# Sixteen-head attention: the row sums from weights whose two key tiles GpSimd has added, and three pieces of work moved in the order

## The chip, the cores and the metric

The kernel runs on one NeuronCore of a Trainium2 chip. A core has TensorE (PE, matrix products into the accumulators, PSUM), VectorE (DVE), ScalarE (ACT), GpSimd (POOL) and SyncE (SP, which here only issues DMAs). Each takes its own list of instructions in order and waits on semaphores for the others. The metric is the device time of one execution in microseconds (us).

## The reference

A decoder of four blocks, each of self-attention, cross-attention and a feed-forward part, on x of 8 batch rows x 256 positions x 256 features. After every part comes `x = layernorm(x + part(x))`. The change touches the self-attention of the first three blocks, parts 0, 3 and 6 of the twelve. All have 16 heads of 16 features:

```python
q, k, v = x @ Wq + bq, x @ Wk + bk, x @ Wv + bv       # split into 16 heads of 16
scores  = q @ k.T * 0.25                              # part 3 adds slope[h] * (j - i), part 6 masks j > i
out     = softmax(scores) @ v                         # per head
x       = layernorm(x + out @ Wo + bo)
```

Part 0 has biases, part 3 (ALiBi) biases and the distance term, part 6 (causal) the mask and no biases. The other nine parts are not touched.

## The kernel before

`attention16` (line 341 on) computes the three parts. A **block** is one batch row b and one half c of the heads (8 heads on 128 partitions, a head in each 16-wide strip), 16 blocks in all, in the order (b, 0), (b, 1). Two blocks of the same b are called a period below.

A block takes four **steps**, units `(e, u)` of `UNITS`. `step(i, s)` puts onto TensorE, alternately, the scores of one unit of the *next* block (tile `s`, queries on the partitions) and the scores of one unit of *this* block turned round (tile `t`, keys on the partitions). The scores `s` serve only to find each query's largest score: VectorE takes the maximum (`dve.tensor_reduce` into `nm`). The turned scores `t` already have that maximum subtracted, through an extra row of the queries (`qm`), so ScalarE takes their exponential straight into `eT` (line 460). An `eT` tile holds, for two heads, two key tiles of 128 keys by 256 queries. In part 6 VectorE first adds the mask and GpSimd clears the half above the diagonal of `eT` (line 466). `s` and `t` are two-bank PSUM tiles of one tag with two buffers, so a step's tiles reuse those of the step before.

`attend(i, e, whats)` multiplies `eT` by the values (`what` 0, `vp`) and by a matrix of ones (`what` 1), the latter giving each query's sum of weights, both into one PSUM tile `av`. For each it runs over k = 0, 1 (the two key tiles) and four heads. Each product of 32-bit data shows as two instructions in the trace, so values are 16 instructions and sums 16. `normalise(i, half)` takes the reciprocal of the sums and multiplies on VectorE, 128 queries at a time, into `aT`.

Around the steps stands work for the neighbours, as filler for TensorE: the projections of the next b (`project_qk` for keys and queries, `proj_tok` for values), the output projection of the last one, the turning of the maxima (`turn_maxima`, `less_max` gives `qm`), the residual (`add_x`; its `xb = x + bo` is GpSimd's), the layer norm (`norm_stats`, with a power on GpSimd, then `norm_scaled`) and the transposition of the new x (`finish`). `leave_qk` brings projected queries or keys out of PSUM, twice each with different strips: on ScalarE in parts 0 and 6, on VectorE in part 3 (`masked`, with `tabs`).

The order on TensorE and VectorE is that of the text: `order_of_text` (line 142) chains every `matmul`, `transpose` and `dve` operation to the one before it on its engine. The lists of ScalarE, GpSimd and SyncE are laid out by the framework's scheduler when the program is built; GpSimd's also holds work of later parts, such as the bias products of part 3 (`bm`, line 816). The loop at lines 526 to 568 is the order around the change; there the functions named above are called between `step(i, 0)` and `step(i, 3)`.

## Time and profile before

| what | value |
|---|---|
| runs | 3790.48, 3794.57, 3794.21 us; median 3794.21 |
| the profiled execution | 3791.73 us, its span 3789.9 us, mean granted TensorE clock 0.978 |
| part 0, 20 to 262 us | busy: TensorE 217.5, VectorE 154.3, ScalarE 99.4, GpSimd 19.7 us |
| part 3, 1040 to 1262 us | TensorE 204.7, VectorE 167.7, ScalarE 70.0, GpSimd 14.1 us |
| part 6, 1770 to 2000 us | TensorE 201.5, VectorE 177.4, ScalarE 80.0, GpSimd 55.9 us |
| products with `vp` and with `ones`, three parts | 1536 instructions each |
| waits of TensorE's scores `s` for the maximum `nm`, 60 to 230 us | 5.5 us in 7 waits |

In the profile's lines a group is given by its line in the kernel, engine, operation, `out<-in` by tile names and shape, then busy time and mean time of one, then the idle time before it and what ended it. Lines 151, 156 and 159 are the helpers through which VectorE's operations and TensorE's products and transpositions go, so there the tile names tell the groups apart. In the timeline a row has its start, its length, the engine (PEld is TensorE's loading of the stationary operand), what it does and, in brackets, the idle time before it and what ended that. The table by stretches gives busy time and number of instructions for PE, PEld, DVE, ACT and POOL, then the granted clock and the share of the DMA engines.

### The profile page before, as it was taken

The page shows a single profiled execution, that of the slowest core. Times are in us where ns is not written, and L with a number is a line of the kernel's source. Part 1 is how long each engine was busy: PE and PEld are TensorE (multiplying, and loading weights), DVE is VectorE, ACT ScalarE, POOL GpSimd, SP SyncE. Part 2 cuts the span into 40 slices and gives each one's busy share as a digit, 9 for nine tenths or more (in the row PEclk, how much of TensorE's full clock was granted, in tenths as well). Part 3 has the DMA queues.
Part 4 walks back from the last instruction along what each step waited for, and adds up shares of the span by engine and source line. Part 5 has one row for each costly group of instructions (what it writes and reads, how often), then busy time and mean ns, then how long its engine had stood idle before and what let it go on. Part 6 is the DMA issues. An engine that isn't in the chain of part 4 may idle for free. (4 is left out here: it accounts for less than half of the span.)

```text
span 3789.9 us, 51235 instructions
## 1 busy us (share of the span) xinstructions
PE 3575.5 (94%) x21130; PEld 2558.6 (68%) x21130; DVE 1730.3 (46%) x3319; ACT 1086.7 (29%) x2615; POOL 853.0 (23%) x900
## 2 busy tenths in 40 slices
PE   7989999999999688999989999999999999999998
PEld 5656555656566465787666766777766777688887
DVE  5753222222478565213874457666664444420003
ACT  3432111111133355322333321343333334321111
POOL 1000000000100366221223320222222333332214
PEclk9998999999999899999999999999999999999999
DMA  7000000001000010342005000100010000035542
GB/s 274 2 15 6 17 17 17 17 17 38 1 1 2 12 56 1 131 164 93 2 2 92 1 23 1 31 1 1 1 31 12 12 11 2 12 131 185 187 164 73
DMA packets 65481, 175.70 MB, mean 46 GB/s; under 512 B 8064, under 2 KB 39552, under 8 KB 52896
## 3 DMA queue, kind: packets, MB, share of 16 engines
q0 software_dynamic: 17280, 98.38, 7.3%
q1 hardware_dynamic: 47968, 74.05, 6.7%
q8 instruction: 166, 2.72, 0.3%
q14 instruction: 67, 0.55, 0.0%
HBM read 139.12 MB, written 33.29 MB: 45 GB/s over the span
## 5 line engine op out<-in xcount | busy, mean ns | idle before, releaser
L151 DVE TENSOR_REDUCE nm<-s 128x4 f32<-128x1024 f32 (+2 forms) x448 | 455.6, 1030 | 154.5 <-PE s L649 66.5
L597 POOL TENSOR_TENSOR ex<-ex,urc 128x1024 f32<-128x1024 f32 x192 | 363.4, 1893 | 717.0 <-DVE urc L151 626.8
L588 ACT ACTIVATE ex<-s,nm 128x256 f32<-128x256 f32 (+1 forms) x704 | 337.8, 494 | 345.7 <-DVE nm L151 327.1
L460 ACT ACTIVATE eT<-t 128x1024 f32<-128x1024 f32 (+1 forms) x192 | 182.6, 953 | 360.3 <-PE t L156 360.3
L797 PE MATMUL pu<-xT_l,w2a 128*128 128x512 f32 x512 | 244.2, 599 | 0.0
L797 PE MATMUL pg<-xT_l,w2a 128*128 128x512 f32 x512 | 242.0, 594 | 1.1 <-ACT sg L922 1.1
L923 DVE TENSOR_TENSOR h<-pu,sg 128x512 f32<-128x512 f32 x128 | 88.6, 692 | 336.6 <-PE pu L797 336.6
L156 PE MATMUL s<-qk,qk 32*128 32x256 f32 (+1 forms) x1536 | 217.2, 400 | 23.7 <-DVE nm L151 17.9
L922 ACT ACTIVATE sg<-pg 128x512 f32<-128x512 f32 x128 | 76.4, 597 | 565.2 <-PE pg L797 565.2
L782 PE MATMUL py<-w2b,h 128*128 128x256 f32 x1024 | 226.2, 379 | 0.0
L159 PE MATMUL etr<-ident,ex 128*128 128x128 f32 x1568 | 215.0, 279 | 10.5 <-issue 7.1
L782 PEld LDWEIGHTS py<-w2b,h 128*128 128x128 f32 x1024 | 194.6, 190 | 40.1 <-issue 15.3
L159 PEld LDWEIGHTS etr<-ident,ex 128*128 128x128 f32 x1568 | 173.4, 142 | 69.8 <-issue 59.4
L156 PE MATMUL t<-qm,qk 32*128 32x256 f32 (+1 forms) x1536 | 204.6, 387 | 10.9 <-DVE nm L151 9.9
L649 PE MATMUL s<-kg,qg 64*128 64x256 f32 x1280 | 192.5, 403 | 3.3 <-DVE eT L151 2.9
L675 PE MATMUL av<-eT,vg 128*64 128x256 f32 x1280 | 189.3, 395 | 4.3 <-DVE eT L151 2.8
L156 PEld LDWEIGHTS s<-qk,qk 32*128 32x128 f32 x1536 | 125.7, 190 | 93.7 <-issue 48.9
L789 DVE SCALAR_TENSOR_TENSOR x<-py,g,x 128x256 f32<-128x256 f32 x256 | 110.2, 478 | 166.1 <-PE py L782 165.9
L797 PEld LDWEIGHTS pu<-xT_l,w2a 128*128 128x128 f32 x512 | 98.1, 192 | 122.1 <-issue 122.1
L797 PEld LDWEIGHTS pg<-xT_l,w2a 128*128 128x128 f32 x512 | 97.0, 191 | 108.0 <-issue 105.0
L1501 PE MATMUL ph<-xgT,w11a 128*128 128x256 f32 x736 | 162.8, 379 | 0.5 <-DVE xgT L1530 0.5
L1508 PE MATMUL py<-w11b,h 128*128 128x256 f32 x736 | 162.6, 379 | 0.0
(339 smaller groups left out, 6227.5 us busy)
## 6 DMA issues: line engine op xcount, KB each, us to landing
slots<-zero SPq DMA_DIRECT2D x16, 1024.0 KB, 16.7
given<-yo SPq DMA_DIRECT2D x23, 256.0 KB, 3.0
w2a<-in_L_ffn_Wg SPq DMA_DIRECT2D x8, 512.0 KB, 4.0
w2a<-in_L_ffn_Wu SPq DMA_DIRECT2D x8, 512.0 KB, 4.8
w2b<-in_L_ffn_Wd SPq DMA_DIRECT2D x8, 512.0 KB, 3.9
lines<-w9r SPq DMA_DIRECT2D x1, 4096.0 KB, 44.4
bias<-lines SPq DMA_DIRECT2D x4, 768.0 KB, 7.5
x<-in_x SPq DMA_DIRECT2D x8, 256.0 KB, 5.5
```

The lines of the kernel that those rows point to most:

```text
L151: return lambda *args, **kw: in_order(getattr(nc.vector, op)(*args, **kw))
L156: in_order(nc.tensor.matmul(*args, **kw))
L159: in_order(nc.tensor.transpose(*args))
L460: nc.scalar.activation(eT[:, :, :n], tt[:, :, :n], AF.Exp)
L588: nc.scalar.activation(ex[:, g, :], flat[:, g, :], AF.Exp, bias=nm[:, g:g + 1], accum_out=sums[:, g:g + 1])
L597: nc.gpsimd.tensor_tensor(ex, ex, rc[:, :nseg].unsqueeze(2).to_broadcast([P, nseg, 1024 // nseg]), ALU.mult)
L649: nc.tensor.matmul(st[:, i, q * S:(q + 1) * S], qg[r:r + d, c, q * P:(q + 1) * P], kg[r:r + d, c, :], start=True, stop=True)
L675: nc.tensor.matmul(av[64 * i:64 * i + d, c * S:(c + 1) * S], vg[:, k, (2 * c + i) * d:(2 * c + i + 1) * d], eT[:, (2 * i + k) * S:(2 * i + ...
L782: nc.tensor.matmul(py[:, q * D:(q + 1) * D], h[:, f, i * P:(i + 1) * P], w2[:, f, :], start=(f == 0), stop=(f == nf - 1))
L797: nc.tensor.matmul(ph, w1[:, c, f * P:(f + 1) * P], xT[p][:, c, :], start=(c == 0), stop=(c == 1))
L1501: nc.tensor.matmul(ph[:, i * S:(i + 1) * S], w1[:, c, f * P:(f + 1) * P], srcs[c], start=(c == 0), stop=(c == 1))
L1508: nc.tensor.matmul(py[:, q * D:(q + 1) * D], h[:, f, q * P:(q + 1) * P], w2[:, f, :], start=(f == 0), stop=(f == NF - 1))
```

## The change

In parts 0 and 3, after each exponential, GpSimd adds the two key tiles of `eT` into a new tile `eS` (four buffers). The sums then need one pass over `eS` in place of two over `eT`. Part 6 keeps its sums over both tiles. In all three parts the order changes:

- the sums of the second strip (e = 1) of a block are taken in the next block: after its step 1 where that has c = 0, after its step 0 where c = 1; before, they followed at the end of a block with c = 1, and after the next block's step 0 for one with c = 0;
- the queries' projection of the next b is cut in its two column halves, one after step 1 of c = 0 (with the sums), one after step 0 of c = 1; `leave_qk` and `masked` take the halves `cs` that are to leave;
- in c = 0 both halves of `normalise` come between step 1 and step 2; in c = 1 they stay around step 1;
- `norm_stats` moves from the end of c = 0 to after step 0 of c = 1, `norm_scaled` after step 1 there.

```diff
@@ -366,31 +366,37 @@
 
             blocks = [(b, c) for b in range(B) for c in range(2)]
             qk = {}
-            qms, avs, eTs, aTs, ys = {}, {}, {}, {}, {}
-
-            def masked(dst, src, i):
+            qms, avs, eTs, eSs, aTs, ys = {}, {}, {}, {}, {}, {}
+
+            def masked(dst, src, i, cs):
 
                 scale = hc[:, 4 + i % 2:5 + i % 2] if i < 2 else hc[:, i % 2:i % 2 + 1]
+                dst = dst[:, cs[0]:cs[-1] + 1, :]
                 if tabs is not None:
-                    dve.scalar_tensor_tensor(dst, src, scale, tabs[:, i], ALU.mult, ALU.add)
+                    dve.scalar_tensor_tensor(dst, src, scale, tabs[:, i, cs[0]:cs[-1] + 1, :],
+                                             ALU.mult, ALU.add)
                 elif kbias is not None:
-                    for c in range(2):
-                        nc.scalar.activation(dst[:, c, :], src[:, c, :], AF.Identity, scale=scale,
+                    for j, c in enumerate(cs):
+                        nc.scalar.activation(dst[:, j, :], src[:, j, :], AF.Identity, scale=scale,
                                              bias=kbias[:, 2 * i + c:2 * i + c + 1])
                 elif i < 2:
                     nc.scalar.activation(dst, src, AF.Copy, scale=scale)
                 else:
                     nc.scalar.activation(dst, src, AF.Identity, scale=scale, bias=hc[:, i:i + 1])
 
-            def project_qk(b, k):
-                pt = proj_T(wk_ if k else wq, xTb(b), 0, f"p{'qk'[k]}_{li}_{b}")
-                return pt.rearrange("p (c s) -> p c s", c=2)
-
-            def leave_qk(b, k, pt):
+            def project_qk(b, k, cs=(0, 1)):
+                pt = bank("mm", f"p{'qk'[k]}_{li}_{b}_{cs[0]}")
+                for j, c in enumerate(cs):
+                    for i, src in enumerate(xTb(b)):
+                        matmul(pt[:, j * S:(j + 1) * S], (wk_ if k else wq)[:, i, c * P:(c + 1) * P],
+                               src, start=(i == 0), stop=(i == 1))
+                return pt[:, :len(cs) * S].rearrange("p (c s) -> p c s", c=len(cs))
+
+            def leave_qk(b, k, pt, cs=(0, 1)):
                 for i in (2 * k, 2 * k + 1):
-                    tg = wk.tile([P, 2, S], F32, tag=f"qk{i}", name=f"qk{i}_{li}_{b}")
-                    masked(tg, pt, i)
-                    qk[b, i] = tg
+                    if (b, i) not in qk:
+                        qk[b, i] = wk.tile([P, 2, S], F32, tag=f"qk{i}", name=f"qk{i}_{li}_{b}")
+                    masked(qk[b, i], pt, i, cs)
 
             def leave_v(b, pv):
                 vp = vpads[b % 2]
@@ -466,6 +472,11 @@
                             nc.gpsimd.affine_select(out=diag, in_=diag, compare_op=ALU.is_ge,
                                                     fill=0.0, base=0, pattern=[[0, 2], [1, P]],
                                                     channel_multiplier=-1)
+                    else:
+
+                        eS = wk.tile([P, 2, S], F32, tag="eS", name=f"eS_{li}_{b2}_{c2}{e2}{u2}", bufs=4)
+                        nc.gpsimd.tensor_tensor(eS, eT[:, :, 0:S], eT[:, :, S:2 * S], ALU.add)
+                        eSs[i, e2, u2] = eS
                     eTs[i, e2, u2] = eT
 
             def turn_maxima(i):
@@ -490,16 +501,18 @@
                     avs[i] = bank("av", f"av_{li}_{b}_{c}")
                 av, vp = avs[i], vpads[b % 2]
                 for what in whats:
-                    for k in range(2):
+                    for k in range(1 if what == 1 and not causal else 2):
                         for j in range(4):
                             h, r = 8 * c + 2 * j + e, 32 * j
                             q0 = P if causal and k == 1 else 0
                             first = e == 0 and what == 0 and k == 0
+                            if what == 1 and not causal:
+                                src = eSs[i, e, j // 2][:, j % 2, :]
+                            else:
+                                src = eTs[i, e, j // 2][:, j % 2, k * S:k * S + S - q0]
                             matmul(av[r:r + 32, what * S + q0:(what + 1) * S],
-                                   vp[:, k, h, :] if what == 0 else ones[:, e, :],
-                                   eTs[i, e, j // 2][:, j % 2, k * S:k * S + S - q0],
-                                   start=first, stop=e == 1 and what == 1 and k == 1,
-                                   skip_group_check=True)
+                                   vp[:, k, h, :] if what == 0 else ones[:, e, :], src,
+                                   start=first, stop=e == 1 and what == 1, skip_group_check=True)
 
             def normalise(i, half):
 
@@ -526,28 +539,37 @@
                 for i, (b, c) in enumerate(blocks):
                     more = b + 1 < B
                     if c == 0:
-                        step(i, 0, lambda: normalise(i - 1, 0))
-                        normalise(i - 1, 1)
+                        step(i, 0)
                         if more:
                             pk = project_qk(b + 1, 1)
                         step(i, 1)
                         if more:
                             leave_qk(b + 1, 1, pk)
-                            pq = project_qk(b + 1, 0)
+                        if i > 0:
+                            attend(i - 1, 1, (1,))
+                        if more:
+                            pq = project_qk(b + 1, 0, (0,))
+                        for half in range(2):
+                            normalise(i - 1, half)
+                        step(i, 2)
+                        if more:
+                            leave_qk(b + 1, 0, pq, (0,))
                     else:
                         step(i, 0)
                         if b > 0:
+                            ys[b - 1] = norm_stats(b - 1, ys[b - 1], f"l{li}")
+                        attend(i - 1, 1, (1,))
+                        if more:
+                            pq = project_qk(b + 1, 0, (1,))
+                        step(i, 1, lambda: normalise(i - 1, 0))
+                        if b > 0:
                             norm_scaled(ys.pop(b - 1))
-                        attend(i - 1, 1, (1,))
-                        step(i, 1, lambda: normalise(i - 1, 0))
                         normalise(i - 1, 1)
                         if more:
+                            leave_qk(b + 1, 0, pq, (1,))
                             pv = proj_tok(wv, xTb(b + 1), 0, f"pv_{li}_{b + 1}")
-                    step(i, 2)
-                    if more:
-                        if c == 0:
-                            leave_qk(b + 1, 0, pq)
-                        else:
+                        step(i, 2)
+                        if more:
                             leave_v(b + 1, pv)
                     attend(i, 0, (0, 1))
                     step(i, 3)
@@ -560,12 +582,11 @@
                         tr = turn_maxima(i + 1)
                         less_max(i + 1, 0, tr)
                     if b > 0 and c == 0:
-                        y = add_x(wk, b - 1, po, bo, f"{li}_{b - 1}")
+                        ys[b - 1] = add_x(wk, b - 1, po, bo, f"{li}_{b - 1}")
                     if i + 1 < len(blocks):
                         less_max(i + 1, 1, tr)
-                    if b > 0 and c == 0:
-                        ys[b - 1] = norm_stats(b - 1, y, f"l{li}")
-                    attend(i, 1, (0,) if c == 0 else (0, 1))
+                    attend(i, 1, (0,))
+                attend(len(blocks) - 1, 1, (1,))
                 for half in range(2):
                     normalise(len(blocks) - 1, half)
                 norm(B - 1, project_out(wk, B - 1, [aTs.pop(B - 1)], wo, bo, f"{li}_{B - 1}"), f"l{li}")
```

## The prediction

> **What bounds the kernel now.** I read the busy table first, then the costliest groups, then the waits of TensorE inside one attention layer, then the timeline of one period there (a period is the two blocks, c = 0 and c = 1, of one batch row).

> ```profile
> PE 3575.5 (94%) x21130; PEld 2558.6 (68%) x21130; DVE 1730.3 (46%) x3319; ACT 1086.7 (29%) x2615; POOL 853.0 (23%) x900
> L151 DVE TENSOR_REDUCE nm<-s 128x4 f32<-128x1024 f32 (+2 forms) x448 | 455.6, 1030 | 154.5 <-PE s L649 66.5
> 90.00:120.00 30.00, 28.57 (x344) 18.20 (x337) 21.36 (x36) 12.89 (x18) 2.21 (x3) 1.00 0.01 2
> ```

> TensorE is the bound over the whole span, and in 30 us of layer 0 it is busy for 28.57, VectorE for 21.36, GpSimd for 2.21. So work taken off TensorE should count, unless VectorE's turn comes: 21.36 of 30 is an average over steps that differ. One period of layer 0, from the timeline:

> ```profile
> 97.34 0.48 PE L156 MATMUL s<-qk,qk 32*128 32x256 f32 x2
> ...
> 98.42 1.07 PE L156 MATMUL av<-eT,vp 128*32 128x256 f32 x16
> ...
> 98.53 1.23 DVE L151 TENSOR_REDUCE nm<-s 128x4 f32<-128x1024 f32 x1 [1.77 <-PE t L156]
> ...
> 99.31 1.05 PE L156 MATMUL av<-eT,ones 128*32 128x256 f32 x16
> 100.28 0.19 PEld L156 LDWEIGHTS s<-qk,qk 32*128 32x128 f32 x2 [0.41 <-issue]
> ...
> 106.14 1.19 DVE L151 TENSOR_REDUCE nm<-s 128x4 f32<-128x1024 f32 x1
> ...
> 107.38 0.48 PE L156 MATMUL s<-qk,qk 32*128 32x256 f32 x2 [0.68 <-DVE nm L151]
> ```

> A step (the scores of the next block beside those of this one) takes TensorE 1.08 us (97.34 to 98.42), its maximum starts on VectorE 1.19 after it began (98.53), and the last line shows that the next step waits for that maximum: it begins 1.24 after the start of that maximum (106.14 to 107.38), 1.27 a step later (109.21 to 110.48), which I use. So two steps are at least 1.19 + 1.27 = 2.46 us apart, and each piece of VectorE work put between two maxima makes that longer. TensorE stands still only where its filler between the steps is shorter. I call the steps of a block S0 to S3, their maxima M0 to M3.

> **What is removed.** Values take 0.89 us (98.42 to 99.31), sums 0.97 (99.31 to 100.28). In layers 0 and 3 each of the sums halves to 0.49; four a period are 1.95 us. The halves of the queries' projection cost together what the whole did, 1.92 (92.42 to 94.34), and only move. Layer 6 (causal) keeps its sums, moved.

> **What the moves cost: layer 0, c = 0** (S0 at 0, all times worked from the rows above and these: half a normalisation 1.20, from 91.48 to 92.68; VectorE free 1.13 after a maximum's start, 92.68 to 93.81). Keys' projection 1.08 to 3.00, S1 at 3.00, M1 at 4.19. Sums and half projection 0.49 + 0.96: S2 at 5.53 instead of 6.00. But both halves of the normalisation, which ran beside S0 and S1, now stand on VectorE between M1 and M2: 5.32 to 7.72. M2 starts at 7.72 where its products were there at 6.72, and S3 follows at 8.99, though TensorE was free at 7.99. Before, S3 came at 8.94. Output projection, turned maxima and values then take 4.28 (100.28 to 104.56) as before: 13.27 against 13.22, so +0.05. All that the block saved is waited away.

> **Layer 0, c = 1.** M0 1.19; statistics 1.08 (105.06 to 106.14) until 3.40; half a normalisation until 4.60, M1 there. S1 at 2.53 (sums 0.49, half projection 0.96), S2 at 5.87. Normalised rows 0.66 and the other half 1.20: M2 at 7.59, S3 at 8.86, M3 10.05; the turned maxima 1.28 after it (114.60 to 115.88), values 0.37 later, the next S0 another 1.00 later: 12.70 against 13.55 (104.56 to 118.11). So -0.85: just the last sums. A full period gains 0.80; six of them (b = 1 to 6) 4.8. In b = 0 no normalisation stands in c = 0 and no statistics in c = 1: S1 to S3 is 4.92 instead of 5.94 (41.69 to 47.63), c = 1 ends about 1.3 earlier, together -2.3. In b = 7, without projections as cover, c = 0 loses 0.45 (S3 at 8.45; before 225.13 to 233.13 = 8.00), c = 1 gives 0.5 back. **Layer 0: -7.1.**

> **Layer 3** does the keys' exit on VectorE too:

> ```profile
> 1109.12 1.23 DVE L151 TENSOR_REDUCE nm<-s 128x4 f32<-128x1024 f32 x1 [0.44 <-PE t L156]
> 1110.27 1.40 DVE L151 SCALAR_TENSOR_TENSOR qk<-pk,hc,w3t 128x512 f32<-128x512 f32 x2
> 1112.12 1.23 DVE L151 TENSOR_REDUCE nm<-s 128x4 f32<-128x1024 f32 x1 [0.46 <-PE t L156]
> ```

> Between M1 and M2 now stand that exit (1.15 after M1, then 1.32 until VectorE takes the next) and the normalisation: M2 at 4.19 + 1.15 + 1.32 + 2.40 = 9.06, S3 at 10.33 where it was 8.94 (1104.94 to 1113.88): +1.39. In c = 1 the queries' second half leaves between M1 and M2 (0.80, as two 256-wide rows of the same kind): 13.50 against 13.54. A period loses 1.35, six lose 8.1; b = 0 gains 2.1; b = 7 as above. **Layer 3: +6.0.**

> **Layer 6.** VectorE's mask and maximum hold it 1.66 (1862.57 to 1864.23), and the next step's second half starts 1.80 after the mask (1862.57 to 1864.37). In c = 0, M1's mask is at 3.72, the normalisation ends at 7.76 and the next mask is there instead of at 6.95: +0.8. In c = 1, 13.93 against 14.30. Six periods +2.5, b = 0 -1.7, b = 7 +0.9: **+1.7.**

> **The new add** is not in the trace. Nearest row: GpSimd's add of two 128x512 tiles, 1.27 us (bias on x); from below 0.8 (two selects of 256 columns, 0.41 each), from above 1.89 (the 1024-wide scaling). I take 1.27, same width and two inputs. In layer 0's c = 0 the exponential of S1 stands behind four keys' exits and ends at 5.95; the sum that needs it is due at 7.50: early with 1.27, 0.4 late with 1.89, and even that hides under the wait for S3 until 8.99. Elsewhere there is more room. 64 adds are 81 us on an engine with 2 to 4 us of work in 30: no throughput limit. The added waits are those of the sums on GpSimd; behind a late one stands the whole of TensorE's order.

> VectorE's rows beside GpSimd work do not lengthen: the maxima stay at 1.22 to 1.23 and the bias add beside the statistics leaves those at 0.42. The pair of row normalisations is 0.41 for 256 columns, like the statistics' 0.41, with no sign of a doubled rate. [...] I take the rows.

> **Sum:** -7.1 + 6.0 + 1.7 = +0.6. On the profiled execution's 3791.73 us (span 3789.9) that is 3792.3; it lies 2.5 below the median of the runs, 3794.21, so I state 3794.8. About 0.2%, 7.6 us, is what a measurement of this kernel can tell from no change.

> **Rivals.** *GpSimd's order, slower.* Its queue is taken in order, and the order is laid out beforehand:

> ```profile
> 26.54 0.25 POOL L854 TENSOR_SCALAR bqs<-c_L_xattn_bq 128x2 f32<-128x2 f32 x1
> 76.66 0.34 POOL L816 TENSOR_TENSOR bm_L_attn_bq<-c_L_attn_bq,hc 128x2 f32<-128x2 f32 x2 [49.87 <-DMA c_L_attn_bq<-in_L_attn_bq]
> ```

> ```profile
> 1848.89 0.22 POOL L184 TENSOR_SCALAR ve_l<-mv_l 128x2 f32<-128x2 f32 x1 [3.13 <-DVE mv_l L151]
> 1849.19 0.71 POOL L186 TENSOR_TENSOR rs_l<-ve_l,nhalf 128x2 f32<-128x2 f32 x1
> 1849.88 0.77 POOL L466 TENSOR_SCALAR_AFFINE_SELECT eT<-eT 128x256 f32<-128x256 f32 x2
> ```

> Layer 3's bias products sit in it 50 us early, waiting for a DMA behind the clearing of the slots. Today that costs nothing. If adds of layer 0 stand behind them, TensorE waits: sums due at 46.1 (first block) get their two adds at 77.6 + 2.5 = 80.1, +34 us; if only those from b = 1 on (due at 69.8), +10. The second fence, from layer 6, shows such a wait already: a select whose exponential was done at 1848.85 starts 1.03 later, behind the statistics' two operations. It decides from the place of the bias products: before the last add that ends ahead of 76.7 or after. For it: the products were placed without regard to the clearing. Against: that place may lie after most of the adds. Middle price +22: 3816.

> *Row statistics behind an add, slower.* If c = 1's second add stands ahead of the 1/sqrt pair on GpSimd, the rows' scale comes at 7.3 instead of 4.7 and VectorE, which wants it at 5.73, loses 1.6 in twelve periods: +19, 3813. Against: the statistics are ready 1.5 us before that add.

> *TensorE bounds every step, faster.* If VectorE's new order were hidden, four halved sums in 14 periods give 27 us: 3767. For it: 28.57 of 30 busy. Against: the 2.46 us between steps, which the shorter fillers (1.38 and 1.45 beside a step's 1.08) just reach with no VectorE work added.

> **Chances.** The balance 0.45 (3787 to 3802 by itself; within 0.2% 0.38, faster 0.03, slower 0.04); GpSimd's order 0.27; row statistics or a longer VectorE chain 0.10; TensorE bound 0.13; the rest, 0.05, mostly within. Faster 0.17, within 0.2% 0.41, slower 0.42. The range runs from the balance's low end, 3786, to the dearest place of the bias products, 3794 + 34 = 3828; it leaves out the fast rival.

> **What would show it.** In the changed profile: layer 0's period 26.0 us, layer 3's 28.1 (26.7 before), layer 6's 27.3; a wait of about 0.9 (layer 0) and 2.3 us (layer 3) of TensorE for the maximum before S3 of c = 0; the adds at 1.27. A single wait of 10 us or more of TensorE for a GpSimd add near 46 to 80 us is the first rival; the rows of x waiting for GpSimd's power are the second. The prediction is wrong if VectorE does not keep the text's order, or if S3 comes without a wait.

## The result, and the profile after

| | before | after |
|---|---|---|
| runs, median | 3794.18 us (4 runs, 3790.48 to 3794.57) | 3815.32 us (4 runs, 3811.0 to 3819.71) |
| the profiled execution | 3791.73 us | 3811.0 us |
| part 0, first product to that of part 1 | 233.55 us | 233.98 us |
| part 3, the same | 248.95 us | 258.61 us |
| part 6, the same | 240.17 us | 247.91 us |
| a full period of layer 0, 3, 6 | 26.76, 26.70, 26.85 us | 26.18, 28.28, 27.44 us, and some longer |

The ratio is 1.0058, 95% interval 1.0041 to 1.0075: slower by 21 us, where 0.6 was forecast. The profiled execution is 19.3 longer: 0.4 in part 0, 9.7 in part 3, 7.7 in part 6, 1.1 gained before part 0, and the rest in parts that the change does not touch. The runs also spread wider than before.

The busy table and the group of the new adds, from the page of the kernel after:

```profile
PE 3564.6 (94%) x20618; PEld 2543.8 (67%) x20618; DVE 1738.4 (46%) x3333; ACT 1091.0 (29%) x2629; POOL 1014.4 (27%) x1028
...
L478 POOL TENSOR_TENSOR eS<-eT 128x512 f32<-128x512 f32 x128 | 162.2, 1269 | 236.9 <-ACT eT L466 236.9
```

TensorE has 512 instructions less and 10.9 us less work, and an add takes 1.27 us, as taken. The work went; the time did not follow. Three views show where it stayed.

**VectorE's order.** Waits of TensorE in layer 3 (1040 to 1262 us): in total, times, longest.

```profile
PE s L156 <- DVE nm L151: 25.5, 16, 2.0
```

The wait for the maximum before S3 of c = 0 is 2.0 us in each period (2.3 forecast), in layer 0 it is 0.40 (0.9 forecast). One of them in the timeline:

```profile
1140.89 0.48 PE L156 MATMUL s<-qk,qk 32*128 32x256 f32 x2 [2.00 <-DVE nm L151]
```

**GpSimd's list.** Its timeline in layer 0, then TensorE's:

```profile
68.00 1.27 POOL L478 TENSOR_TENSOR eS<-eT 128x512 f32<-128x512 f32 x1 [2.30 <-ACT eT L466]
76.27 0.34 POOL L837 TENSOR_TENSOR bm_L_attn_bq<-c_L_attn_bq,hc 128x2 f32<-128x2 f32 x2 [7.00 <-DMA c_L_attn_bq<-in_L_attn_bq]
...
77.18 2.48 POOL L478 TENSOR_TENSOR eS<-eT 128x512 f32<-128x512 f32 x2
```

```profile
79.72 0.64 PE L156 MATMUL av<-eS,ones 128*32 128x256 f32 x8 [3.41 <-POOL eS L478]
80.29 1.92 PE L156 MATMUL pq<-xT_in,w0a 128*128 128x256 f32 x4
82.14 0.80 PE L156 MATMUL s<-qk,qk 32*128 32x256 f32 x2
```

Two adds are in line behind part 3's bias products, which wait for their DMA until 76.27. TensorE's sums wait 3.41 us for them, and then TensorE itself is slow: 1.92 us for a half projection that takes 1.13 in the other periods. That period is 31.31 us instead of 26.18.

**The clock.** The table by stretches of 3.41 us in layer 3, busy times of PE, PEld, DVE, ACT and POOL, then the granted clock:

```profile
1138.62:1142.03 3.41, 1.41 (x25) 0.78 (x17) 2.97 (x5) 0.01 (x1) 1.26 (x1) 1.00 0.00 0
1142.03:1145.44 3.41, 3.41 (x10) 2.64 (x9) 1.23 (x1) 1.02 (x1) 1.26 (x1) 0.50 0.00 0
1145.44:1148.86 3.42, 3.42 (x45) 1.83 (x44) 2.35 (x4) 0.76 (x1) 1.27 (x1) 1.00 0.00 0
1155.68:1159.10 3.42, 1.73 (x20) 1.14 (x20) 2.98 (x6) 1.12 (x2) 0.64 (x2) 1.00 0.00 0
1159.10:1162.51 3.41, 3.31 (x38) 2.13 (x39) 1.68 (x4) 1.02 (x2) 1.26 (x1) 1.00 0.00 0
```

In the first stretch lies the 2.0-us wait, and TensorE is busy for 1.41 us only. In the whole of the next the clock is at half, and in it stands the output projection, 3.68 us instead of 1.99. Then the clock is full again. After the fourth row, a stretch with 1.73 busy, the clock stays full. The period with the half-clock stretch is 29.97 us, its neighbours 28.28. Every period of layer 3 has the 2.0-us wait, but only two of six have a half-clock stretch; in the trace of before none of its six has one.

### The profile page after: what moved, and what is told of

Read it like the earlier page. It is cut to its first block, busy times and chain, and to the rows that moved or that the text cites. A ratio compares the mean times of both kernels' runs of the same rounds, so it can differ in the third digit from the quotient of the medians.

```text
span 3809.3 us, 50431 instructions
## 1 busy us (share of the span) xinstructions
PE 3564.6 (94%) x20618; PEld 2543.8 (67%) x20618; DVE 1738.4 (46%) x3333; ACT 1091.0 (29%) x2629; POOL 1014.4 (27%) x1028
## 5 line engine op out<-in xcount | busy, mean ns | idle before, releaser
L151 DVE TENSOR_REDUCE nm<-s 128x4 f32<-128x1024 f32 (+2 forms) x448 | 455.9, 1031 | 170.4 <-PE t L156 76.1
L466 ACT ACTIVATE eT<-t 128x1024 f32<-128x1024 f32 (+1 forms) x192 | 182.6, 952 | 364.6 <-PE t L156 363.9
L156 PE MATMUL s<-qk,qk 32*128 32x256 f32 (+1 forms) x1536 | 216.7, 401 | 42.2 <-DVE nm L151 38.1
L478 POOL TENSOR_TENSOR eS<-eT 128x512 f32<-128x512 f32 x128 | 162.2, 1269 | 236.9 <-ACT eT L466 236.9
L159 PE MATMUL etr<-ident,ex 128*128 128x128 f32 x1568 | 215.2, 280 | 10.5 <-issue 7.1
L156 PE MATMUL t<-qm,qk 32*128 32x256 f32 (+1 forms) x1536 | 205.8, 388 | 18.3 <-DVE nm L151 17.7
L159 PEld LDWEIGHTS etr<-ident,ex 128*128 128x128 f32 x1568 | 173.5, 142 | 69.8 <-issue 59.4
L156 PEld LDWEIGHTS s<-qk,qk 32*128 32x128 f32 x1536 | 125.8, 192 | 113.6 <-DVE nm L151 66.5
L184 POOL TENSOR_SCALAR ve_l<-mv_l 128x2 f32<-128x2 f32 x104 | 23.0, 222 | 532.0 <-DVE mv_l L151 531.2
```

The lines of the kernel that those rows point to most:

```text
L151: return lambda *args, **kw: in_order(getattr(nc.vector, op)(*args, **kw))
L156: in_order(nc.tensor.matmul(*args, **kw))
L159: in_order(nc.tensor.transpose(*args))
L466: nc.scalar.activation(eT[:, :, :n], tt[:, :, :n], AF.Exp)
```

## The experiments

Three theories stood at the start. **A**: VectorE's order and GpSimd's list cost what the change lost. **B**: the adds themselves cost it. **C**: there was nothing to gain. D (VectorE's rows wait for an add of GpSimd) and E (the clock's stretches) came out of the first four runs. Times are compared by the ratio to the kernel before in the same set of runs; in two of the four sets every kernel, the one before too, took some 30 us longer, of which the traces put 21 to 26 us into the last part of the decoder.

| run | ratio, 95% | layer 0 | layer 3 | layer 6 | half-clock loss, layers 3 and 6 |
|---|---|---|---|---|---|
| before | 1 | 26.76 | 26.70 | 26.85 | 0 and 7.5 |
| after | 1.0058 [1.0041, 1.0075] | 26.18 | 28.28 | 27.43 | 3.4 and 11.0 |
| after_again | 1.0070 [1.0056, 1.0083] | 26.18 | 28.28 | 27.63 | 5.1 and 21.5 |
| moves_only | 1.0019 [1.0009, 1.0029] | 26.20 | 27.92 | 27.43 | 0 and 11.0 |
| adds_only | 0.9992 [0.9982, 1.0001] | 26.84 | 26.35 | 27.76 | 0 and 18.2 |
| early_cols | 1.0038 [1.0024, 1.0052] | 26.18 | 28.29 | 27.69 | 5.1 and 21.6 |
| split_norm | 0.9979 [0.9970, 0.9988] | 25.71 | 27.35 | 26.37 | 0 and 13.1 |
| adds_stt | 1.0030 [1.0018, 1.0042] | 27.04 | 26.55 | 27.05 | 0 and 13.4 |
| adds_stt_early | 1.0002 [0.9993, 1.0011] | 27.04 | 26.55 | 27.04 | 0 and 12.5 |
| fill_stalls | 1.0030 [1.0018, 1.0041] | 26.18 | 28.28 | 28.14 | 0 and 2.5 |
| skip_one_early | 0.9974 [0.9963, 0.9984] | 26.32 | 25.84 | 26.84 | 1.7 and 7.6 |
| skip_one_fill | 0.9968 [0.9956, 0.9980] | 26.33 | 25.84 | 26.84 | 0 and 5.3 |
| split_early_fill | 0.9961 [0.9948, 0.9975] | 25.71 | 27.34 | 26.36 | 0 and 1.9 |
| mixed | 0.9907 [0.9890, 0.9923] | 25.71 | 25.84 | 26.37 | 0 and 2.3 |

Periods are in us of the profiled executions, the most frequent one in layers 0 and 3; in layer 6, where half-clock stretches fall into many, the full one least touched by them (in adds_only every one has such a stretch). The last column sums (1 - granted clock), in us, from 25 us after the start of part 3 to 20 before its end, and from 25 us after the start of part 6 to its end, in steps of 1 us.

### One half of the change each: adds_only and moves_only

adds_only has the order of the kernel before, with the adds and the halved sums:

```diff
+                    else:
+                        eS = wk.tile([P, 2, S], F32, tag="eS", name=f"eS_{li}_{b2}_{c2}{e2}{u2}", bufs=4)
+                        nc.gpsimd.tensor_tensor(eS, eT[:, :, 0:S], eT[:, :, S:2 * S], ALU.add)
...
-                    for k in range(2):
+                    for k in range(1 if what == 1 and not causal else 2):
...
```

> The order of the kernel before, with the adds on GpSimd and the halved sums and nothing moved. Theory A (VectorE's new order between the maxima and GpSimd's full queue cost what the change loses): four sums of 0.49 us less in a period on TensorE, of which about 1.4 show (the sums after step 0 of c = 1 stand beside the normalised rows on VectorE and may give nothing), so layers 0 and 3 each lose about 10 us, and the bias products of part 3, which stand behind the tenth add in GpSimd's list as they do in the changed kernel, give 5 back in part 0: 3776 to 3783 us. Theory B (the adds themselves, late or in the way of VectorE, eat the saving, and the moves are free): about 3815, as the changed kernel. Theory C (the maxima already bound every step of the old order too): -0.5 a period, about 3792.

moves_only has the new order without the adds, with these lines taken out again.

> The changed kernel's order without the adds, the sums over both key tiles as before. Theory A: the steps wait for VectorE anyway, so sums of 0.97 instead of 0.49 us are mostly hidden, and there is no wait for GpSimd in part 0: layer 0's period about 26.3 us (changed kernel 26.18), layer 3's 28.3 to 28.5 (28.28), layer 6's 27.4 (27.44); in all 3810 to 3818 us. Theory B: the moves are free, 3794, periods 26.8, 26.7 and 26.9 as in the kernel before.

The moves alone cost 0.19%: layers 3 and 6 get longer, layer 0 shorter by 0.56 us a period. That lies between the theories, whose times stand for ratios of 1.004 to 1.006 (A) and 1.000 (B). The adds then gain nothing on top of them: layer 0 is 26.18 with and 26.20 without, layer 3 even 28.28 with and 27.92 without. What TensorE saves there, it waits for, as theory A says. In layer 3 the wait before S3 of c = 0 shows it, in moves_only:

```profile
1136.97 0.48 PE L156 MATMUL s<-qk,qk 32*128 32x256 f32 x2 [1.14 <-DVE nm L151]
```

It is 1.14 us without the adds and 2.00 with them, and only with them has layer 3 half-clock stretches. So the work that was taken off TensorE made the wait long enough for them. But adds_only was to gain 11 to 18 us and gained nothing that can be told (layer 0: 26.84 against 26.76), so A's figure for it fell, and B has a part in it. (In this trace part 6, whose instructions are those of the kernel before, also loses 18.2 us to half clock where before lost 7.5; how much of the missing gain that is in the median can't be said from one trace.) The timeline of adds_only shows what:

```profile
133.80 0.71 POOL L186 TENSOR_TENSOR rs_l<-ve_l,nhalf 128x2 f32<-128x2 f32 x1
134.48 1.26 POOL L471 TENSOR_TENSOR eS<-eT 128x512 f32<-128x512 f32 x1
134.54 1.67 DVE L151 TENSOR_SCALAR x<-y,mv_l,rs_l 128x256 f32<-128x256 f32 x2
```

The two normalised rows start 0.06 us after an add and end 0.47 after its end: 1.67 us, where they take 0.73 alone. Groups of VectorE in layer 0 (50 to 250 us): busy, then mean ns of one. First the kernel before, then after, then adds_only:

```profile
L151 DVE TENSOR_REDUCE nm<-s 128x4 f32<-128x1024 f32 x57 | 69.6, 1220 | 36.8 <-PE t L156 24.5 <-PE s L156 12.0
...
L151 DVE TENSOR_SCALAR x<-y,mv_l,rs_l 128x256 f32<-128x256 f32 x14 | 5.2, 410 | 1.3 <-POOL rs_l L186 1.1
```

```profile
L151 DVE TENSOR_REDUCE nm<-s 128x4 f32<-128x1024 f32 x56 | 68.5, 1223 | 39.3 <-PE t L156 39.3
...
L151 DVE TENSOR_SCALAR x<-y,mv_l,rs_l 128x256 f32<-128x256 f32 x14 | 9.7, 733 | 0.0
```

```profile
L151 DVE TENSOR_REDUCE nm<-s 128x4 f32<-128x1024 f32 x56 | 68.4, 1221 | 29.7 <-PE t L156 21.0 <-PE s L156 8.3
...
L151 DVE TENSOR_SCALAR x<-y,mv_l,rs_l 128x256 f32<-128x256 f32 x14 | 12.7, 945 | 5.0 <-POOL rs_l L186 4.9
```

Those maxima, reciprocals and statistics of the kernel after that stand beside an add take 1.22, 0.95 and 0.39 to 0.42 us, and those that stand clear of one 1.22 to 1.23, 0.94 to 0.96 and 0.40 to 0.42; only the write of x from y grows. (The residuals never met an add.) In the kernel after it meets the last 0.61 us of one: 1.08 us a pair in the steady periods, which again ends 0.47 after the add. In moves_only, the same order without adds, the pair takes 0.73.

### early_cols: GpSimd's list

```diff
+    early = {n: load_cols(n, k) for n, k in (("L1_attn_bq", 2), ("L1_attn_bk", 2), ("L1_xattn_gains", 10))}
```

loaded at the start, and used where the columns were loaded before.

> The changed kernel, with the bias columns of part 3 and the gains of part 4 loaded at the start, so that the products made of them no longer stand in GpSimd's list with a DMA behind the clearing of the slots to wait for. Theory A (that list held TensorE once, at 76 to 80 us): the period of b = 1 falls from 31.4 to 26.2 us, 3810 us, 5 below the changed kernel. Rival (the long period came from the clock or from the adds, not from the wait for the DMA): 3815, the period of b = 1 still above 28.

The mechanism is shown. Waits of TensorE from 62 to 89 us of the kernel after, and from 55 to 85 us of early_cols:

```profile
PE av L156 <- POOL eS L478: 3.4, 1, 3.4
PE s L156 <- DVE nm L151: 0.4, 1, 0.4
```

```profile
PE ntr L160 <- DVE nm L152: 1.3, 1, 1.3
PE s L157 <- DVE nm L152: 1.1, 2, 0.7
```

No wait for an add is left, the period of b = 1 is 26.18 instead of 31.31 us, and part 0 is 5.6 us shorter than after. (This wait is not the same in each run: in after_again that period is 27.81, in adds_only 30.58.) Whether the time shows it can't be told: 1.0038 against 1.0058, with intervals that overlap, and in the profile part 6 took back 9.2 us in half-clock stretches. Of the periods of layer 6, five are 30.3 to 30.7 us. The table by stretches there:

```profile
1866.75:1870.16 3.41, 1.98 (x18) 1.39 (x18) 2.27 (x4) 1.29 (x2) 0.77 (x2) 1.00 0.00 0
1870.16:1873.57 3.41, 3.41 (x34) 2.09 (x34) 0.91 (x3) 0.00 (x0) 0.00 (x0) 0.50 0.02 5
...
1897.47:1900.89 3.42, 2.11 (x21) 1.42 (x22) 2.14 (x4) 1.29 (x2) 0.77 (x2) 1.00 0.00 0
1900.89:1904.30 3.41, 3.41 (x34) 2.26 (x34) 1.10 (x3) 0.15 (x1) 0.00 (x0) 0.50 0.00 0
```

In this trace (read from its clock in stretches of 0.1 us) drops in layers 3 and 6 begin at 1136.30, 1194.33, 1225.05, 1808.72, 1822.38, 1839.44, 1870.16, 1900.89 and 1931.61 us, among others: whole multiples of 3.4133 us apart, to 0.02 us, and each lasts one such stretch. So in this trace the stretches lie on one grid. In layer 3 of it and of after, every stretch with TensorE busy for 1.62 us or less was followed by one of half clock, none with 1.71 or more (in after 1.41 and 1.42 against 1.72 and more): the 2.0-us wait counts there by how much of one stretch it empties. In layer 6 the half-clock stretches followed stretches with 2.2 or less, but some with as little as 2.03 were followed by full clock, and in after 2.15 stood before both: the busy time is not quite what decides. The last four starts are 30.72 us apart, nine stretches: a period with its half-clock stretches nearly fills nine, so the next period meets the grid at almost the same place and is slow again.

A wait of 2.0 us in layer 3, and of 1.26 in layer 6 (before 1821.09 in early_cols), was enough for a half-clock stretch; what sets the clock beyond that, no run shows.

### split_norm: the two halves between M1 and M2

```diff
-                        for half in range(2):
-                            normalise(i - 1, half)
-                        step(i, 2)
+                        normalise(i - 1, 0)
+                        step(i, 2, lambda: None)
+                        normalise(i - 1, 1)
```

The empty function is what `step` has without it.

> The changed kernel, with one half of the normalisation of c = 0 before step 2 as now and the other behind step 2's maximum, in all three layers. Theory A (two halves between M1 and M2 make S3 late): in layer 0 the wait of 0.9 before S3 goes, -5.7 in six periods; in layer 3 S3 comes 1.2 earlier, -7.2, and with the 2-us wait gone the half-speed output projections of 3.68 us go too, -3.4; in layer 6 0.8 a period, -5, and its slow periods, up to -5: 3790 to 3798 us, periods 25.2, 27.1 and 26.6. Rival (the wait only moves, to M3 or to the output projection that needs the second half): 3812 or more, periods within 0.3 of the changed kernel's.

Theory A held. The wait before S3 of c = 0 is gone in layers 0 and 6, and in layer 3 it is 0.81 us instead of 2.00; its sum there, in the waits from 1040 to 1262 us, against the 25.5 of the kernel after:

```profile
PE s L156 <- DVE nm L151: 16.1, 14, 1.5
```

With the long wait the half-clock projections of layer 3 went, and part 3 is 9.9 us shorter than after. In layer 3 the period gains 0.93 of the 1.2 expected, in layer 6 1.07 where 0.8 was. In layer 0 it is 0.47 and not 0.95: the forecast had taken TensorE to be free a whole microsecond before S3. In the kernel after, halved sums take 0.57 us (from 159.90 to the next row at 160.47) and the half projection 1.06 (to 161.53), not 0.49 and 0.96, so less wait was there to win.

### adds_stt and adds_stt_early: another form for the rows

```diff
-            dve.tensor_scalar(xs[b][:, q, :], y[:, q, :], mv[:, q, 0:1], rs[:, q:q + 1],
-                                    ALU.subtract, ALU.mult)
+            dve.scalar_tensor_tensor(xs[b][:, q, :], y[:, q, :], mv[:, q, 0:1],
+                                     rs[:, q:q + 1].to_broadcast([P, D]), ALU.subtract, ALU.mult)
```

> The order of the kernel before with the adds (as adds_only, whose normalised rows took 1.67 us beside an add that started just ahead of them, where they take 0.73 alone), but the rows are normalised with the three-operand form, the row's 1/sqrt spread over the columns as a tensor. Theory D (VectorE's form with two per-row numbers can't run while GpSimd adds two tensors; the three-operand form can): the pair takes 0.8 to 0.9 us beside the add, the period of layer 0 falls from 26.84 to about 26.0 and that of layer 3 from 26.35 to about 25.5; 10 us in all, a ratio of 0.996 to the kernel before. Rival (the rows wait for GpSimd's power, or every VectorE operation is slowed by an add): the pair stays at 1.6 or more, the periods and the ratio (0.999) stay.

> adds_stt, with the bias columns of part 3 and the gains of part 4 loaded at the start. If GpSimd's full list is a second, separate cost of the adds: the period of b = 1 in layer 0, 30.6 in adds_only, comes down to that of the others, 4 to 5 us in all, a ratio of 0.994 to 0.995 to the kernel before. If both costs hide one another: as adds_stt.

The form does not help: the pair takes 0.88 us alone and 1.88 beside the add, again as long as the add and its own last part. The ratio, 1.0030, lies above both forecasts: the pair is longer than in adds_only, and the period of b = 1 is 33.69 us. That it is the form with two per-row numbers fell; that the pair lasts until after the add's end stands, in both forms (1.88 and 1.67 us beside it, 0.88 and 0.73 alone). What in the two engines holds it up, no run shows. The early columns bring the period of b = 1 from 33.69 to 27.06 and the ratio from 1.0030 to 1.0002, 10.5 us, of which 6.6 are that period: here their gain shows in the time, but not the 0.994 to 0.995 that was expected.

### fill_stalls: useless work, and the change again

```diff
+            def fill(i, n):
+                b, c = blocks[i]
+                for k in range(n):
+                    for j in range(4):
+                        matmul(avs[i][32 * j:32 * j + 32, 0:S], none, qk[b, 0][:, c, :],
+                               start=False, stop=False, skip_group_check=True)
...
                     attend(i, 0, (0, 1))
+                    if li in (3, 6) and c == 0 and b > 0:
+                        fill(i, 2)
+                    if li == 6 and c == 1:
+                        fill(i, 1)
                     step(i, 3)
...
+                        if li == 6:
+                            fill(i, 1)
                         tr = turn_maxima(i + 1)
```

`none` is a tile of zeros.

> The changed kernel with useless work on TensorE: products with a matrix of zeros, added to the accumulators (they change no value), 0.9 us before step 3 of c = 0 in layers 3 and 6, 0.45 before step 3 of c = 1 and before the turned maxima in layer 6; some 20 us of products in all, each at most as long as the wait it stands in. Theory E (the clock halves for one window of 3.41 us when TensorE was busy for less than about 1.7 us, in layer 6 about 2.2, of the window before; the windows lie on a fixed grid): no half-clock window in layer 3's six periods and none in layer 6's, 28.28 and 27.4 to 27.6 in every period, 5 to 7 windows of 1.71 us gained: about 10 us less than the changed kernel. Rival (the drops come by chance or with load, not from idle time): as many drops as before, the time the same or up to 20 us longer.

> The changed kernel once more, on the chip of these three, for its periods and its half-clock windows there. Periods 26.2, 28.3 and 27.4 where no window is slow, a ratio of 1.004 to 1.007 to the kernel before. If the slow windows depend on where the grid lies when the kernel starts, their number in layers 3 and 6 (8 in the first profile) differs, and the time with it by 1.71 us each.

Layer 6 from 1790 to 1990 us, first the change again, then with the useless products (PE busy and its instructions first, the clock third from the end):

```profile
1790.00:1990.00 200.00, 176.58 (x2003) 122.15 (x2001) 146.61 (x284) 72.57 (x130) 47.46 (x122) 0.91 0.01 1
```

```profile
1790.00:1990.00 200.00, 185.72 (x2398) 124.59 (x2394) 155.91 (x300) 75.68 (x134) 49.86 (x128) 1.00 0.01 2
```

Theory E held, and with a change that only adds work: no half-clock stretch is left in the periods of layers 3 and 6, every full period of layer 3 is 28.28 us, and the kernel takes 3804.47 us where the change takes 3818.12 on the same chip, 13.7 less. Layer 6's period is 28.15 in place of an undisturbed 27.44, so the products cost 0.7 a period there and still won. after_again met the grid elsewhere than the first profile: 12 half-clock stretches in part 6, beside the one at its start, where there were 6, and three lengthened periods in layer 3 where there were two. So the place of the grid, which no line of the kernel sets, went in layer 6 with 21.5 us of half-clock loss in the one profile and 11.0 in the other.

### skip_one_early, skip_one_fill, split_early_fill, mixed: the costs taken away

skip_one_early is adds_only with the early columns, less the one add that stands beside the rows; its heads sum over both tiles (shown against adds_only):

```diff
-                    else:
+                    elif (c2, s) != (1, 0):
                         eS = wk.tile([P, 2, S], F32, tag="eS", name=f"eS_{li}_{b2}_{c2}{e2}{u2}", bufs=4)
...
-                    for k in range(1 if what == 1 and not causal else 2):
+                    for k in range(2):
                         for j in range(4):
+                            if k == 1 and what == 1 and (i, e, j // 2) in eSs:
+                                continue
```

> The order of the kernel before with the adds and the early columns, but without the add that stands beside the normalised rows: the exponential of step 0 of each block with c = 1 is not added, its two heads take their sums over both key tiles as before (0.24 us more on TensorE in a period). Theory D (a VectorE operation that writes x from y waits while GpSimd adds two tensors): the pair of normalised rows is back at 0.73 us, the period of layer 0 falls from 26.84 to 25.9 to 26.1, that of layer 3 from 26.35 to 25.4 to 25.7, ten microseconds under the order with all adds: a ratio of 0.995 to 0.997 to the kernel before. Rival (the rows are late for another reason, the 1/sqrt on GpSimd or the statistics): the pair is short but starts later, and the periods stay; ratio 0.999 to 1.000.

skip_one_fill puts one `fill` before the last sums and one before the turned maxima of c = 1, in layer 6.

> skip_one_early with products with zeros (no value changes) in the causal layer 6 alone: 0.45 us before the last sums and 0.45 before the turned maxima of blocks with c = 1, where TensorE waits 1.1 and 0.8 us for VectorE. Theory E (a window of 3.41 us that is idle for too long halves the clock of the next): the 5 to 7 half-clock windows of layer 6 go to 0 or 1, its period is 26.9 to 27.2 in every period: 6 to 10 us below skip_one_early, a ratio of 0.993 to 0.995. If the fills come where TensorE doesn't wait, up to 6 us longer instead.

split_early_fill is split_norm with the early columns and, in layer 6, one `fill` before step 3 and one before the turned maxima of c = 1.

> The changed kernel's order with three repairs: the second half of the normalisation of c = 0 behind step 2's maximum, the early columns, and in layer 6 products with zeros before step 3 and before the turned maxima of c = 1 (0.45 us each, no value changes). If the three losses (VectorE's chain, GpSimd's list, half-clock windows) are separate and make up what the change lost: layer 0 at 25.7 in every period, layer 3 at 27.35, layer 6 at 26.4 to 26.7 with no half-clock window; 10 to 16 us below the kernel before, a ratio of 0.996 to 0.997. If they overlap, or the change loses elsewhere: 0.999 or more.

mixed is split_early_fill, but layer 3 runs in the order of the kernel before, with every add but the one.

> Each layer in the order that was faster in it: layers 0 and 6 as in split_early_fill (25.7 and 26.4 us a period), layer 3 in the order of the kernel before with all adds but the one beside the normalised rows (25.84 in skip_one_early instead of 27.34). If the layers are independent, layer 3 gives six times 1.5 us and 7 to 9 in all below split_early_fill: a ratio of 0.9935 to 0.9945 to the kernel before, about 3768 us where that one has 3792. If what is saved in one layer comes back as half-clock windows in another: 0.996 or more.

The rows in skip_one_early, group of layer 0 (50 to 250 us):

```profile
L152 DVE TENSOR_SCALAR x<-y,mv_l,rs_l 128x256 f32<-128x256 f32 x14 | 5.1, 410 | 1.3 <-POOL rs_l L187 1.1
```

They are back at 410 ns, and with the adds now out of their way the order of the kernel before gains: 0.9974, just short of the 0.995 to 0.997 expected. Theory D is shown by taking the meeting away. The period fell by 0.5 and not 0.7 to 0.9, in part since the sums over mixed tiles take the full 0.97 us (137.56 to 138.53 in its timeline, where those of adds_only take 0.54). skip_one_fill rids layer 6's full periods of half-clock stretches (27.13 in the first, 26.85 in the others), but these had been few in skip_one_early. Its 0.9968 misses the 0.993 to 0.995 expected, and the intervals of the two overlap: what the filling gained there is unclear. split_early_fill shows the three losses to be separate: all three layers at the forecast periods, 0.9961. mixed takes each layer's better order, 0.9907 [0.9890, 0.9923], under the 0.9935 to 0.9945 forecast, 34 us under the kernel before in the same set; it beats both kernels. Against the first trace of before, 23 of these lie ahead of the last part; whether the rest is the kernel's or the set's is open. Its busy table:

```profile
PE 3561.6 (94%) x20770; PEld 2539.8 (67%) x20770; DVE 1733.0 (46%) x3319; ACT 1091.4 (29%) x2629; POOL 1005.0 (26%) x1023
```

TensorE is as busy as after (3564.6) with the useless products in it: what mixed gains is waits and half clock, not work.

## Why the prediction was wrong in size

The forecast was a balance (+0.6) and the range held the result; the time lies 20 above the balance. That the range held it is partly luck: it reached so far up for a wait of 10 to 34 us in GpSimd's list, and that list cost 5.1. Step by step:

- **Layer 3, +6.0 forecast, 9.7 measured.** The period was right: 28.28 against 28.1, from the keys' exit and two half normalisations between M1 and M2. moves_only (27.92) and split_norm (27.35) show that chain. That 28.28 came so near is helped by 0.35 of the rows' meeting with an add (below), which the sum did not have. Of the missing 3.7 us, 3.4 are two half-clock stretches of 1.7. The step that failed priced a wait at its own length only.
- **Layer 0, -7.1 forecast, +0.4 measured.** The period was right within 0.21 (26.18 against 25.97). Of the 7.5, 5.1 are one period: 3.41 us of wait for adds behind the bias products, and 1.71 of half clock after it. That is the first rival in its place, at half its lower price of 10, and without the mark that was given for it, a single wait of 10 us or more: the products stand behind the tenth add. early_cols shows it. Most of the rest is the next point.
- **The rows against the add.** "I take the rows", which priced this meeting at nothing, was the wrong choice. The pair grows from 0.73 to 1.08, M1 to M2 of c = 1 from the forecast 2.99 to 3.33, six times in each of two layers, about 4 us. In parts 0 and 3 the trace of before has no such meeting: GpSimd's only add of this width there stood beside statistics, which took 0.42 and 0.40 us as ever. But it has one later, with GpSimd's 1024-wide scaling, that the prediction did not read:

```profile
2232.12 1.89 POOL L597 TENSOR_TENSOR ex<-ex,urc 128x1024 f32<-128x1024 f32 x1
2232.18 2.30 DVE L151 TENSOR_SCALAR x<-y,mv_l,rs_l 128x256 f32<-128x256 f32 x2 [0.76 <-POOL rs_l L186]
```

The pair takes 2.30 us in place of 0.73 and ends 0.47 after GpSimd's operation, as it does after the adds. So "VectorE's rows beside GpSimd work do not lengthen" was read from other operations than the one that mattered.

- **Layer 6, +1.7 forecast, 7.7 measured.** Period 27.44 against 27.3. The half-clock stretches cost 11.0 in place of 7.5 us in this profile; in after_again 21.5. The remaining 2.5 us are not taken apart.
- **The halved pieces.** 0.49 and 0.96 us were taken, 0.54 to 0.57 and 1.06 measured. This hid under VectorE's waits, so the end of c = 0 still came out (13.19 against 13.27).
- **Row statistics behind an add** did not come: in the steady periods they run ahead of the second add. **TensorE bounds every step** is refuted by moves_only, whose sums over both tiles left layer 0's period at 26.20.

So the mechanism of the balance held, and one of its rivals beside it. What made the larger part of the 21 us was a cost that no part of the prediction had: half-clock stretches after waits. (1 - granted clock), summed over the whole profiled execution, is 85.4 us before and 97.3 after: 11.9 more, at most that much of the 19.3.

## What to carry to other kernels

Work taken off the busiest engine counts only where no other engine's result is awaited there: here layer 0's period was 26.18 us with the sums halved and 26.20 without. Find the chain between two waits and count what each move puts into it, and look at what stands ahead of a new operation in an engine laid out in order (here 3.41 us of wait). A wait of TensorE can cost more than itself, here up to 1.71 us more after waits of 1.26 and 2.0 us: look at the granted clock in stretches of 3.41 us behind it, and fill it, with useless products if need be (13.7 us less in fill_stalls). Before an add goes to GpSimd, see which VectorE operations will run at the same time, and look for a row of the same kind that GpSimd has already lengthened.
